# The last four blocks of a conditional-adapter kernel: b2 of block 126 by TensorE, block 125's last step by ScalarE and GpSimd, and two results stored in halves

## The chip, the cores and the metric

The kernel runs on one core of one Trainium2 chip. The metric is the time of one execution on the device in microseconds (us); lower is better. Three runs of the kernel before the change took 308.55, 308.73 and 308.92 us, so the median is 308.73 us. The core's engines are named as in the profile: PE is TensorE's matmuls and PEld its weight loads, DVE is VectorE, ACT is ScalarE, POOL is GpSimd, and SP is SyncE, which here only issues DMAs. "SPq" and "ACTq" stand for the instruction queues of SP and ACT when they issue a DMA.

## The reference

The input `x` holds 128 blocks of 128 rows by 512 columns in float32. Each block `b` has a language id from 0 to 9, and the id picks the block's own weights, biases, gamma and beta out of ten:

```
w1, w2 = W1[language_ids], W2[language_ids]
h = relu(einsum('bsh,bha->bsa', x, w1) + b1[language_ids][:, None, :])
adapted = einsum('bsa,bah->bsh', h, w2) + b2[language_ids][:, None, :]
y = x + adapted
mean = mean(y, axis=-1); var = mean(square(y - mean), axis=-1)
normed = (y - mean) * rsqrt(var + 1e-5)
out = x + normed * gamma[language_ids][:, None, :] + beta[language_ids][:, None, :]
```

H is 512, the inner width A is 128. All biases, gamma and beta are drawn, so none of them can be left out. One block's result is 128 x 512 float32, 256 KB, and the whole output is 33.55 MB.

## The kernel before, in words

The program is one loop over the 128 blocks, software-pipelined by hand: in iteration `i` TensorE transposes x of block `i`, multiplies block `i-1` with W1 ("down") and block `i-2` with W2 ("up"), and the other engines work on block `b = i-3` and its predecessors. Every instruction is put into its engine's queue by `keep`, which chains it behind the engine's last one, so the order within each engine is the order in which the program text is run. Between engines there are semaphore waits, which the framework adds from the tiles that each instruction reads and writes. Two engines that touch the same PSUM tile are ordered as well, also where both only read it.

The work on one block, with the lines that the profile names:

- TensorE: transposes (L235), `down` (L258), `up` (L275). For the blocks that `b2_by_matmul` names (5 and 127), a small bf16 matmul ahead of `up` puts b2 of the block into the PSUM tile first (L274).
- GpSimd: for the blocks that neither `b2_by_matmul` nor `b2_by_vector` names, `r = x + b2` (L245); for each block `o = x + beta` (L252), which starts the output tile.
- VectorE: `residual` (L292) adds `r`, or `x` itself where b2 is already in, to the PSUM tile and sums the rows; `scale` (L358) subtracts the mean and multiplies by gamma; `finish` (L367, and L424 in the tail) multiplies by the reciprocal deviation and adds the result to `o`.
- ScalarE: the square with its row sum (L315, in the tail L399), then an approximate reciprocal root (L325) that three small VectorE instructions refine (L329, L331, L334). ScalarE also copies xT and W1 and does the relu.

Row sums and means are kept for pairs of blocks: a [128, 2] tile `sums` for blocks 2g and 2g+1, and one small instruction, in the tail `negative_means` on VectorE (L299), for both means. It names the first block's PSUM tile as a second operand and does not use its values.

The last blocks are done by a tail of its own. `E` is 123. In the tail each block has its own deviation (`deviation_of`: square and root on ScalarE; `rstd_of(b, 1..3)`: the three steps on VectorE). Block 123 and 124 are finished by `by_pool`: ScalarE applies mean and deviation to the PSUM tile and writes `n` to SBUF (L413), GpSimd multiplies by gamma (L415) and adds `o` (L417). Block 125 is scaled on VectorE; its last step is shared: VectorE's `finish_cols` does columns 128 to 511 (L424), ScalarE and GpSimd columns 0 to 127 (L413, L417). Blocks 126 and 127 are finished by VectorE, 127 in two halves. Stores of single blocks (`store_last`, L420) are issued by SP, but those of 124 and 125 by ScalarE, behind its last computation. GpSimd's additions `x + beta` of blocks 124 to 127 stand behind `r` of block 126 in its queue, and the steps of `by_pool` behind them.

The part that the change touches is the call `tail(126)`, which runs after `up(127)` and lists the rest of the program in one order:

Of the kernel before, what the change touches and what calls it, by code (L numbers as in the profile page):

```python
# [12 lines left out]
ALU = mybir.AluOpType  # L13
# [13 lines left out]
def cond_resid_kernel(ctx: ExitStack, tc: tile.TileContext, x, itok, W1, b1, W2, b2, gamma, beta, out):  # L27
# [8 lines left out]
    nc = tc.nc  # L36
    B, S, H = x.shape
# [8 lines left out]
    def keep(ins):  # L46

        engine = ins.ins.engine
        if engine in last:
            tc.add_manual_dep(ins.ins, last[engine], behind, reason="kept order")  # L50
        last[engine] = ins.ins.name
        return ins
# [14 lines left out]
    E = B - 5  # L67
# [145 lines left out]
    xT, hT, rs, os, ys, ssqs, nmeans, rstds = {}, {}, {}, {}, {}, {}, {}, {}  # L213
# [1 line left out]


    def b2_by_matmul(b):
        return b in (5, B - 1)

    def b2_by_vector(b):  # L220
        return b < 4 or 8 <= b < B - 8 and (b % 4 == 1 if b < 24 else b % 16 in (1, 6, 11) or b % 32 == 30)
# [56 lines left out]
    def col(tiles, b):  # L278

        return tiles[b // 2][:, b % 2 : b % 2 + 1]  # L280
# [14 lines left out]
    def negative_means(g):  # L295

        nmeans[g] = st.tile([P, 2], FP, tag="nmean", name=f"nmean_{g}")
        keep(
            nc.vector.scalar_tensor_tensor(  # L299
                nmeans[g], sums[g], -1.0 / H, ys[2 * g][:, 0:2], ALU.mult, ALU.bypass  # L300
            )
        )
# [52 lines left out]
    def scale(b):  # L355
        v = lid(b, ET.DVE)
        keep(
            nc.vector.scalar_tensor_tensor(  # L358
                ys[b], ys[b], col(nmeans, b), gamma_b[:, bass.ds(v * H, H)], ALU.add, ALU.mult
            )  # L360
        )
# [15 lines left out]


    shifts = {}

    def of_one(b):
        if -b not in parts_of:
            pool, tag = {E + 3: (p_h, "h"), E + 4: (p_x, "xT")}.get(b, (p_s, "s"))
            parts_of[-b] = pool.tile([P, 1], FP, tag=tag, name=f"root_of_{b}"), st.tile([P, 1], FP, tag="part", name=f"part_of_{b}")
        return parts_of[-b]
# [10 lines left out]
    def deviation_of(b):  # L396
        ssqs[b] = st.tile([P, 1], FP, tag="ssq", name=f"ssq_{b}")
        sq = tp.tile([P, H], FP, tag="sq", name=f"sq_{b}")
        keep(nc.scalar.activation(sq, ys[b], AF.Square, bias=col(sums, b), scale=-float(H), accum_out=ssqs[b]))  # L399
        root(ssqs[b], of_one(b)[0])  # L400
# [8 lines left out]
    def by_pool(b, scaled, cols=slice(0, H)):  # L409

        n = rp.tile([P, H], FP, tag="r", name=f"n_{b}")[:, cols]
        bias = 0.0 if scaled else shifts[b]
        keep(nc.scalar.activation(n, ys[b][:, cols], AF.Identity, bias=bias, scale=rstd_col(b)))  # L413
        if not scaled:
            keep(nc.gpsimd.tensor_tensor(n, n, gamma_b[:, bass.ds(lid(b, ET.Pool) * H, H)], ALU.mult))  # L415
        o = os[b // 2][:, b % 2, cols]
        keep(nc.gpsimd.tensor_tensor(o, n, o, ALU.add))  # L417

    def store_last(b, engine=nc.sync, cols=slice(0, H)):
        keep(engine.dma_start(out=out[b][:, cols], in_=os[b // 2][:, b % 2, cols]))  # L420

    def finish_cols(b, cols=slice(0, H)):
        o = os[b // 2][:, b % 2, cols]
        keep(nc.vector.scalar_tensor_tensor(o, ys[b][:, cols], rstd_col(b), o, ALU.mult, ALU.add))  # L424

    def tail(b):
        p = E // 2
        residual(b)
        if b == E + 1:
            rstd(p, 1)  # L430
            scale(E - 1)
            rstd(p, 2)
            finish(E - 2)
            store(p - 1)
            rstd(p, 3)
            deviation_of(b)
            shift(E)
            by_pool(E, False)
        elif b == E + 2:
            rstd_of(b - 1, 1)  # L440
            negative_means(b // 2)
            rstd_of(b - 1, 2)
            finish_cols(E - 1)
            store_last(E - 1)
            rstd_of(b - 1, 3)
            store_last(E)
            deviation_of(b)
        elif b == E + 3:
            left, right = slice(0, H // 2), slice(H // 2, H)
            few, most = slice(0, H // 4), slice(H // 4, H)  # L450
            shift(b - 2)
            by_pool(b - 2, False)
            residual(b + 1)
            rstd_of(b - 1, 1)
            scale(b - 1)
            negative_means(b // 2)
            rstd_of(b - 1, 2)
            deviation_of(b)
            scale(b)
            rstd_of(b - 1, 3)  # L460
            rstd_of(b, 1)
            deviation_of(b + 1)
            rstd_of(b, 2)
            finish_cols(b - 1, most)
            by_pool(b - 1, True, few)
            store_last(b - 2, nc.scalar)
            store_last(b - 1, nc.scalar)
            rstd_of(b, 3)
            rstd_of(b + 1, 1)
            finish_cols(b)  # L470
            store_last(b)
            rstd_of(b + 1, 2)
            scale(b + 1)
            rstd_of(b + 1, 3)
            for cols in (left, right):
                finish_cols(b + 1, cols)
                store_last(b + 1, nc.sync, cols)
# [45 lines left out]
    for i in range(3, B + U):  # L523
        b = i - U - 1
# [111 lines left out]
```

## Time and profile before

| | us |
|---|---|
| median of three runs | 308.73 |
| lowest and highest run | 308.55 and 308.92 |
| span of the profiled execution, first to last instruction | 306.5 |
| PE busy | 294.6 |
| DVE busy | 295.9 |
| ACT busy | 282.3 |
| POOL busy | 283.9 |

The profile's page gives the profiled execution's span, 306.5 us, and no other time for it; the median of the runs is 2.23 us longer than that span. All four computing engines are busy for 92 to 97% of the span, on average over a long steady part and a short beginning and end. The change lies wholly in the end, the last 16 us. How to read the rows that follow: a row of the timeline has the start in us from the span's start, the length in us, the engine, the line, the operation, the tiles written and read, the shape, and in brackets the idle time of the engine before it and what ended that. A row of the chain of waits has start, length and what was being done or waited for. The numbers of blocks are not in the rows; they follow from the order. A row of DMA issues ends with the median time from issue to landing.

### The profile page before, as it was taken

How to read it: one execution, taken by the hardware profiler on the slowest of the kernel's cores; microseconds unless marked ns; L12 is line 12 of the kernel's file. 1: busy time of each engine (PE TensorE's matmuls, PEld its weight loads, DVE VectorE, ACT ScalarE, POOL GpSimd, SP SyncE). 2: the span in 40 equal slices, each digit the busy share in tenths (PEclk: the TensorE clock that was granted, in tenths of full speed). 3: DMA queues.
4: the chain of work that ended last, by engine and by line, in shares of the span. 5: the costliest groups of instructions: out<-in, count | busy, mean ns of one | idle time of the engine just before them, and what ended most of it. 6: DMA issues, size and time to landing. Idle time of an engine off the chain costs nothing. (4 is left out here: it accounts for less than half of the span.)

```text
span 306.5 us, 6981 instructions
## 1 busy us (share of the span) xinstructions
PE 294.6 (96%) x1835; PEld 220.0 (72%) x1835; DVE 295.9 (97%) x771; ACT 282.3 (92%) x777; POOL 283.9 (93%) x238
## 2 busy tenths in 40 slices
PE   8999999999999999999999999999999999999960
PEld 3748787777777777777777777777777777777730
DVE  6889999999999999999999999999999999999985
ACT  3858999999999999999999999999999999999981
POOL 1349899999999999999999999999999999999994
PEclk9999999999999999999999999999999999999995
DMA  6999999976678766766777666767776666773324
GB/s 231 379 390 388 373 371 354 387 231 240 221 255 276 250 202 241 226 257 219 259 276 243 213 209 238 265 224 260 275 238 206 226 231 242 246 266 137 135 109 171
DMA packets 43769, 77.85 MB, mean 254 GB/s; under 512 B 1961, under 2 KB 7348, under 8 KB 43730
## 3 DMA queue, kind: packets, MB, share of 16 engines
q1 hardware_dynamic: 43382, 76.84, 72.1%
q10 hardware_dynamic: 348, 0.57, 0.5%
q8 instruction: 15, 0.25, 0.3%
q14 instruction: 24, 0.20, 0.2%
HBM read 43.85 MB, written 33.55 MB: 253 GB/s over the span
## 5 line engine op out<-in xcount | busy, mean ns | idle before, releaser
L252 POOL TENSOR_TENSOR o<-x,beta_b 128x512 f32<-128x512 f32 x128 | 173.9, 1395 | 10.2 <-DVE beta_b L211 9.5
L245 POOL TENSOR_TENSOR r<-x,b_b 128x512 f32<-128x512 f32 x97 | 135.7, 1399 | 7.3 <-DVE b_b L211 6.2
L258 PE MATMUL ph<-xT,w1s 128*128 128x128 f32 x1024 | 135.4, 275 | 0.0
L275 PE MATMUL py<-w,hT 128*128 x256 | 131.2, 595 | 0.5 <-DVE b_b L211 0.5
L258 PEld LDWEIGHTS ph<-xT,w1s 128*128 128x128 f32 x1024 | 124.9, 192 | 1.0 <-ACT hT L266 0.5
L235 PEld LDWEIGHTS pxT<-ident,x 128*128 128x128 f32 x512 | 66.6, 151 | 65.3 <-issue 49.2
L358 DVE SCALAR_TENSOR_TENSOR py<-py,nmean,gamma_b 128x512 f32<-128x512 f32 x126 | 95.0, 754 | 0.9 <-ACT sq L399 0.8
L367 DVE SCALAR_TENSOR_TENSOR o<-py,rstd,o 128x512 f32<-128x512 f32 x122 | 91.2, 748 | 0.0
L315 ACT ACTIVATE sq<-py,sum 128x512 f32<-128x512 f32 x124 | 85.9, 693 | 2.8 <-DVE py L292 2.5
L235 PE MATMUL pxT<-ident,x 128*128 128x128 f32 x512 | 78.2, 276 | 0.0
L239 ACT COPY xT<-pxT 128x512 f32<-128x512 f32 x128 | 74.7, 584 | 3.5 <-PE pxT L235 3.5
L292 DVE SCALAR_TENSOR_TENSOR py<-py,r 128x512 f32<-128x512 f32 x97 | 67.0, 691 | 0.2
L226 ACT COPY w1s<-w 128x512 f32 x107 | 65.5, 612 | 0.0
L266 ACT ACTIVATE hT<-ph,b1T 128x128 f32<-128x128 f32 x128 | 46.9, 366 | 7.9 <-PE ph L258 2.6
L275 PEld LDWEIGHTS py<-w,hT 128*128 128x128 f32 x256 | 39.1, 192 | 2.9 <-issue 1.0
L315 ACT ACTIVATION_READ_ACCUMULATOR sq<-py,sum 128x1 f32 x124 | 25.0, 202 | 0.0
L292 DVE SCALAR_TENSOR_TENSOR py<-py,x 128x512 f32<-128x512 f32 x31 | 21.7, 699 | 0.4
L285 DVE TENSOR_TENSOR py<-py,b_b 128x512 f32<-128x512 f32 x29 | 20.2, 695 | 0.7 <-PE py L275 0.6
L325 ACT ACTIVATE root<-ssq,eps 128x2 f32<-128x2 f32 x62 | 16.4, 265 | 0.0
L292 DVE DVE_READ_ACCUMULATOR py<-py,r 128x1 f32 x97 | 13.7, 141 | 0.0
L306 ACT ACTIVATE nmean<-sum 128x2 f32<-128x2 f32 x62 | 12.3, 198 | 0.0
L329 DVE SCALAR_TENSOR_TENSOR part<-ssq,root 128x2 f32<-128x2 f32 x62 | 9.3, 151 | 0.2 <-ACT root L325 0.2
(55 smaller groups left out, 90.4 us busy)
## 6 DMA issues: line engine op xcount, KB each, us to landing
out_dram<-o SPq DMA_DIRECT2D x61, 512.0 KB, 3.4
x<-in_x_dram SPq DMA_DIRECT2D x29, 1024.0 KB, 6.2
x<-in_x_dram SPq DMA_DIRECT2D x6, 512.0 KB, 8.8
w1e<-in_L_cond_W_dram SPq DMA_DIRECT2D x2, 1280.0 KB, 12.3
w<-in_L_cond_W_dram SPq DMA_DIRECT2D x4, 640.0 KB, 8.1
w1s<-in_L_cond_W_dram SPq DMA_DIRECT2D x9, 256.0 KB, 8.4
w<-in_L_cond_W_dram SPq DMA_DIRECT2D x1, 1792.0 KB, 10.3
w<-in_L_cond_W_dram SPq DMA_DIRECT2D x1, 768.0 KB, 5.4
```

What stands on the lines that cost most here:

```text
L226: keep(nc.scalar.copy(w1s[b].rearrange("p k a -> p (k a)"), src))
L235: keep(nc.tensor.transpose(pxs[b][:, k, :], cols, ident))
L239: keep(nc.scalar.copy(xT[b], pxs.pop(b)))
L245: keep(nc.gpsimd.tensor_tensor(rs[b], xb(b), b2_b[:, bass.ds(v * H, H)], ALU.add))
L252: keep(nc.gpsimd.tensor_tensor(os[g][:, j, :], xb(b), beta_b[:, bass.ds(v * H, H)], ALU.add))
L258: nc.tensor.matmul(phs[b], lhsT=w1s[b][:, k, :], rhs=xT[b][:, k, :], start=(k == 0), stop=(k == KC - 1))
L266: keep(nc.scalar.activation(hT[b], phs.pop(b), AF.Relu, bias=b1T[:, bass.ds(lid(b, ET.Activation), 1)]))
L275: keep(nc.tensor.matmul(ys[b], lhsT=hT[b], rhs=w2[:, bass.ds(v * H, H)], start=not m, stop=True))
L292: nc.vector.scalar_tensor_tensor(ys[b], ys[b], 1.0, r, ALU.mult, ALU.add, accum_out=col(sums, b))
L315: nc.scalar.activation(sq, ys[b], AF.Square, bias=col(sums, b), scale=-float(H), accum_out=col(ssqs, b))
L358: nc.vector.scalar_tensor_tensor(ys[b], ys[b], col(nmeans, b), gamma_b[:, bass.ds(v * H, H)], ALU.add, ALU.mult)
L367: nc.vector.scalar_tensor_tensor(o, ys.pop(b), rstds[g][:, j : j + 1], o, ALU.mult, ALU.add)
```

## The change

There are four edits.

1. Block 126 joins 5 and 127 in `b2_by_matmul`. GpSimd no longer makes `r` for block 126, TensorE issues one more small matmul before `up(126)`, and VectorE's residual of block 126 reads `x`.
2. In `tail(126)`, `negative_means` of the pair 126 and 127 moves from ahead of `deviation_of(126)` (square and root of block 126) to behind it.
3. `finish_cols` of block 125 on VectorE goes away; `by_pool(125, True)` now does all 512 columns on ScalarE (one instruction instead of 128 columns) and GpSimd.
4. For blocks above 123, that is 124 and 125, `by_pool` makes GpSimd's last addition in two instructions of 256 columns each, and the stores of 124 and 125 on ScalarE's queue are issued in halves too: four stores of 128 KB instead of two of 256 KB.

```
     def b2_by_matmul(b):
-        return b in (5, B - 1)
+        return b in (5, B - 2, B - 1)
...
+    halves = slice(0, H // 2), slice(H // 2, H)
...
     def by_pool(b, scaled, cols=slice(0, H)):
...
-        o = os[b // 2][:, b % 2, cols]
-        keep(nc.gpsimd.tensor_tensor(o, n, o, ALU.add))
+        for part in halves if b > E else (cols,):
+            keep(nc.gpsimd.tensor_tensor(os[b // 2][:, b % 2, part], n[:, part], os[b // 2][:, b % 2, part], ALU.add))
...
             scale(b - 1)
-            negative_means(b // 2)
             rstd_of(b - 1, 2)
             deviation_of(b)
+            negative_means(b // 2)
             scale(b)
             rstd_of(b - 1, 3)
             rstd_of(b, 1)
             deviation_of(b + 1)
             rstd_of(b, 2)
-            finish_cols(b - 1, most)
-            by_pool(b - 1, True, few)
-            store_last(b - 2, nc.scalar)
-            store_last(b - 1, nc.scalar)
+            by_pool(b - 1, True)
+            for part in halves:
+                store_last(b - 2, nc.scalar, part)
+            for part in halves:
+                store_last(b - 1, nc.scalar, part)
             rstd_of(b, 3)
```

In this part of `tail`, `b` is 126. `few` and `most` (columns 0 to 127 and 128 to 511) are still defined, but no longer used.

## Prediction

> **What bounds the kernel now.** I read the page's head first, then the chain of waits from 299 us on, then the timeline of each engine over the last 16 us, and last the DMA views. All edits lie behind 290 us, and up to there the order on every engine is the same before and after, so only the end can change the time.
>
> ```profile
> span 306.5 us, 6981 instructions
> ```
>
> ```profile
> 301.69 0.42 POOLq L631
> ...
> 302.17 0.48 DVE o L424
> 302.65 0.39 DVEq L631
> ```
>
> The chain names GpSimd's end (302.11) as what released VectorE's last step, the two halves of block 127 at 302.17 and 302.57. I don't follow it there. The timeline of VectorE shows a nearer cause.
>
> ```profile
> 295.58 0.69 DVE L292 SCALAR_TENSOR_TENSOR py<-py,r 128x512 f32<-128x512 f32 x1
> ...
> 296.37 0.70 DVE L292 SCALAR_TENSOR_TENSOR py<-py,x 128x512 f32<-128x512 f32 x1
> ...
> 297.72 0.15 DVE L299 SCALAR_TENSOR_TENSOR nmean<-sum,py 128x2 f32<-128x2 f32 x1
> ...
> 298.73 0.76 DVE L358 SCALAR_TENSOR_TENSOR py<-py,nmean,gamma_b 128x512 f32<-128x512 f32 x1 [0.78 <-ACT sq L399]
> 299.39 0.15 DVE L334 SCALAR_TENSOR_TENSOR rstd<-part_of,root_of 128x1 f32<-128x1 f32 x1
> 299.46 0.15 DVE L329 SCALAR_TENSOR_TENSOR part_of<-ssq,root_of 128x1 f32<-128x1 f32 x1
> 299.64 0.16 DVE L331 SCALAR_TENSOR_TENSOR part_of<-part_of,root_of 128x1 f32<-128x1 f32 x1
> 299.73 0.62 DVE L424 SCALAR_TENSOR_TENSOR o<-py,rstd,o 128x384 f32<-128x384 f32 x1
> 300.26 0.15 DVE L334 SCALAR_TENSOR_TENSOR rstd<-part_of,root_of 128x1 f32<-128x1 f32 x1
> ...
> 300.51 0.75 DVE L424 SCALAR_TENSOR_TENSOR o<-py,rstd,o 128x512 f32<-128x512 f32 x1
> ...
> 301.90 0.15 DVE L334 SCALAR_TENSOR_TENSOR rstd<-part_of,root_of 128x1 f32<-128x1 f32 x1
> ```
>
> In order these are the residuals of 126 and 127, the means of their pair, the scaling of 126, the third step for 125, the first two for 126, the finish of 125 (columns 128 to 511), the third step for 126, the finish of 126, and the third step for 127. From 300.26 to the finish at 300.51 are 0.25 us, from 301.90 to 302.17 are 0.27: the last finish waits for VectorE's own step just as the one before it does, and GpSimd's end is a coincidence. So VectorE is busy without a gap from 298.73 to 303.04, and its start there hangs on ScalarE:
>
> ```profile
> 294.12 0.78 ACT L413 ACTIVATE n<-py,shift,rstd 128x512 f32<-128x512 f32 x1
> ...
> 296.50 0.78 ACT L413 ACTIVATE n<-py,shift,rstd 128x512 f32<-128x512 f32 x1 [0.38 <-DVE shift L407]
> 297.91 0.69 ACT L399 ACTIVATE sq<-py,sum 128x512 f32<-128x512 f32 x1 [0.64 <-DVE nmean L299]
> ...
> 299.72 0.27 ACT L325 ACTIVATE root_of<-ssq,eps 128x1 f32<-128x1 f32 x1
> 300.38 0.37 ACT L413 ACTIVATE n<-py,rstd 128x128 f32<-128x128 f32 x1 [0.40 <-DVE o L424]
> ```
>
> ScalarE makes n of 123 and 124, the square of 126 (idle 0.64 us for the means), the root of 127, and n of 125 (idle 0.40 for VectorE's finish of 125). The square doesn't use the means. It only reads the same PSUM tile as they do, and the same holds for n of 125 and the finish.
>
> Behind the last computation come the stores:
>
> ```profile
> 300.75:302.00 1.25, 0.50 0.00 0
> 302.00:305.00 3.00, 0.50 0.95 349
> ```
>
> ```profile
> 301.29 0.33 SPq L420 DMA_DIRECT2D out_dram<-o  x1
> ...
> 301.72 0.89 ACTq L420 DMA_DIRECT2D out_dram<-o  x2
> ...
> 303.10 0.59 SPq L420 DMA_DIRECT2D out_dram<-o  x1
> ```
>
> ```profile
> out_dram<-o SPq DMA_DIRECT2D x2, 256.0 KB, 2.0
> ...
> out_dram<-o SPq DMA_DIRECT2D x2, 128.0 KB, 2.3
> ```
>
> The columns of the first fence are window, length, TensorE's clock, DMA share and GB/s. No DMA runs from 300.75 to 302.00, then four blocks' results (1.05 MB: 126, 124, 125, and 127 in halves) leave at 349 GB/s until 305.0. The last store is issued at 303.10 and lands 2.3 us later, at 305.4, though it is only half as large as the stores that landed in 2.0. It stands in line behind the others. The span ends 1.1 us after that landing. So two things set the end: VectorE's last step, and 3 us of stores that all begin at 302.
>
> **The change, part by part.** *The square ahead of the means.* The square of 126 can start when n of 124 is done, 296.50 + 0.78 = 297.28, instead of 297.91. Scaling began 0.82 us after the start of the square (298.73 − 297.91) because it overwrites what the square reads. That would put it at 298.10. But in the new order the means wait for the square, and scaling needs the means. One small VectorE step behind another takes 0.18 us (299.46 to 299.64), so scaling starts at 298.28: 0.45 us earlier.
>
> The Trainium skill, page "PSUM — Partial Sum Buffer", section "PSUM bank collisions raise a hardware error", says that two engines must not touch one bank in the same partitions at the same time, two readers included, so that software has to order them. The trace agrees with its 0.64 us wait of a reader for a reader. By this rule the means wait and the sum below holds; without it they would stay at 297.72 and the end would come 0.18 us earlier still.
>
> *The finish of 125 leaves VectorE.* From the second step for 126 to its third are now 0.62 us (299.64 to 300.26), with the finish in between; without it they take 0.18. That is 0.44 earlier. The finish of 126 moves from 300.51 to 299.62, and what follows on VectorE is unchanged, so its end goes from 303.04 to 302.15: 0.89 us. ScalarE keeps up: root of 127 at 299.72 − 0.63 = 299.09, done at 299.36, and its first use was at 300.32 − 0.89 = 299.43 by the same shift.
>
> *n of 125 in one piece on ScalarE.* It needs the third step for 125, at 299.39 − 0.45 + 0.15 = 299.09, and ScalarE, free at 299.36. It takes 0.78 like the other n, until 300.14.
>
> *b2 of 126 by TensorE.* The nearest rows:
>
> ```profile
> 28.28 0.38 PE L274 MATMUL py<-parts,pick 96*128 96x512 bf16 x1
> 28.50 1.02 PE L275 MATMUL py<-w,hT 128*128 x2
> ```
>
> ```profile
> 293.96 1.02 PE L275 MATMUL py<-w,hT 128*128 x2
> 294.95 0.38 PE L274 MATMUL py<-parts,pick 96*128 96x512 bf16 x1
> 295.21 1.13 PE L275 MATMUL py<-w,hT 128*128 x2
> ```
>
> The small matmul costs 0.22 (block 5) to 0.26 us (block 127) between starts. Block 126's product, done at 294.98, moves to 295.20 or 295.24. VectorE takes it at 295.58, so 0.34 us of cover is left; if the cover were gone, all that follows would shift by the excess. Block 127's product is done at 296.34 and taken at 296.37, so there is no cover: its residual moves by 0 to 0.26 us. That is late for the means alone (297.72 to 297.98 at most), which now wait for the square until 298.10. I count nothing.
>
> *GpSimd.*
>
> ```profile
> 290.20 1.46 POOL L245 TENSOR_TENSOR r<-x,b_b 128x512 f32<-128x512 f32 x1
> 291.43 1.45 POOL L252 TENSOR_TENSOR o<-x,beta_b 128x512 f32<-128x512 f32 x1
> ...
> 296.34 1.45 POOL L415 TENSOR_TENSOR n<-n,gamma_b 128x512 f32<-128x512 f32 x1
> ...
> 299.08 1.26 POOL L415 TENSOR_TENSOR n<-n,gamma_b 128x512 f32<-128x512 f32 x1
> ...
> 300.43 1.27 POOL L417 TENSOR_TENSOR o<-n,o 128x512 f32<-128x512 f32 x1
> 301.65 0.46 POOL L417 TENSOR_TENSOR o<-n,o 128x128 f32<-128x128 f32 x1
> ```
>
> Without r of 126 all behind it moves up by 1.23 us (290.20 to 291.43). The multiplication for 123 moves to 295.11 (n is ready at 294.90), that for 124 to 297.85 (n ready at 297.28), the addition for 124 to 299.20. No row shows an addition of 256 columns. It lies between 0.46 and 1.27; in proportion to the columns between these two it is 0.73, which I take, as both ends are the same operation. The halves of 124 are then done at 299.93 and 300.66, those of 125 (n ready at 300.14) at 301.39 and 302.12. With 1.27 each the last would be at 304.3, with 0.46 GpSimd would wait for n and end at 301.1.
>
> *Stores.* ScalarE issues the halves of 124 at 300.14 (behind n of 125) and 300.66, those of 125 at 301.39 and 302.12; one issue takes 0.89 / 2 = 0.45, so they don't hold each other up. SP issues 126 at 301.29 − 0.89 = 300.40 and the last half of 127 at 303.10 − 0.89 = 302.21. Bytes flowed 0.71 us behind the first issue (301.29 to 302.00), so now from 300.85, and the same 1.05 MB at the same 349 GB/s take 3.0 us, to 303.85 if the line never runs empty. Landing comes 0.4 behind the bytes (305.0 to 305.4): 304.25. Another bound is the last issue: with the old delay of 2.3 it lands at 304.5, alone with half of a 256 KB store's 0.75 us saved from the 2.0 at 303.85. I take 304.3, 1.1 us earlier than now.
>
> **Sum.** 305.4 to 304.3 is −1.1 us; the span becomes 305.4. The profiled span is 2.23 us below the median of 308.73, and I leave that difference as it is: 307.6 us. The mechanism's own range is 307.2 (last store alone, 303.85) to 307.8 (old delay, 304.5).
>
> **Rivals.** *GpSimd's end decides*, as the chain reads it: VectorE's last finish waits for 302.12 instead of 302.11, and the time stays at 308.7. The 0.25 and 0.27 us above speak against it. *A wider GpSimd half*: at 1.27 each the last half store is issued at 304.3, and lands 1.7 us later at 306.0, 0.6 later than now: 309.3, slower. It needs more than 1.1 us per half to lose; the 128-column row at 0.46 speaks against it. *Partial loss*: a store line that starts early but runs empty, or TensorE's extra matmul with more than its 0.34 us of cover, would leave a gain of 0.3 to 0.6: 308.3.
>
> *Halved stores cost more than they bring.* If a half took as long on the DMA engines as a whole (0.75 us), the six halves and one whole would need 5.25 us from 300.85, land at 306.5 and give 309.8, slower. From 0.57 us per half on it is slower than now. The line of 302 to 305 with two halves in it still ran at 349 GB/s, which is 0.38 per half. The Trainium skill, page "DMA: Bandwidth & Descriptors", section "Rules for kernel authors", tells to coalesce small transfers into a large one, and so speaks for this rival. The 2.3 us of a 128 KB store beside 2.0 of a 256 KB one agree with it only on the face, since the later ones stood in line.
>
> **Chances.** The forecast 0.79; GpSimd's end 0.04; partial loss 0.09; a wide GpSimd half 0.03; dear halved stores 0.05. A measurement of this kernel can tell about 0.2%, 0.6 us, from no change. Faster is the forecast, 0.79; the same is GpSimd's end and the partial loss, 0.13; slower is the rest, 0.08. For 8 in 10 the range reaches from 307.2 into the partial loss, 308.4.
>
> **What would show it.** Right: the square of 126 follows n of 124 without idle time; the means follow the square and scaling starts near 298.3; VectorE ends near 302.1; the DMA share is high from about 300.9 to 303.9. Wrong: idle time of VectorE before the residual of 126, GpSimd halves over 0.9 us, a last store that lands over 2.5 us behind its issue, or a last finish that still starts just behind GpSimd's end.

## The result, and the profile after

The changed kernel takes 307.26 us (median of five runs, 306.69 to 307.67) where the kernel before takes 308.73 on the same chip (five runs, 308.48 to 308.97). The ratio is 0.9951, with a 95% interval of 0.9939 to 0.9963. The prediction was 307.6, faster. The profiled execution has a span 1.2 us shorter than that of before:

```profile
span 305.3 us, 6987 instructions
```

VectorE's timeline, from the residual of 126 on (the columns are those of the rows in the prediction):

```profile
295.61 0.69 DVE L292 SCALAR_TENSOR_TENSOR py<-py,x 128x512 f32<-128x512 f32 x1
...
296.39 0.70 DVE L292 SCALAR_TENSOR_TENSOR py<-py,x 128x512 f32<-128x512 f32 x1
...
297.74 0.15 DVE L331 SCALAR_TENSOR_TENSOR part_of<-part_of,root_of 128x1 f32<-128x1 f32 x1
298.00 0.16 DVE L299 SCALAR_TENSOR_TENSOR nmean<-sum,py 128x2 f32<-128x2 f32 x1
298.19 0.76 DVE L358 SCALAR_TENSOR_TENSOR py<-py,nmean,gamma_b 128x512 f32<-128x512 f32 x1
...
299.10 0.15 DVE L331 SCALAR_TENSOR_TENSOR part_of<-part_of,root_of 128x1 f32<-128x1 f32 x1
299.29 0.15 DVE L334 SCALAR_TENSOR_TENSOR rstd<-part_of,root_of 128x1 f32<-128x1 f32 x1
299.36 0.15 DVE L329 SCALAR_TENSOR_TENSOR part_of<-ssq,root_of 128x1 f32<-128x1 f32 x1
299.55 0.75 DVE L425 SCALAR_TENSOR_TENSOR o<-py,rstd,o 128x512 f32<-128x512 f32 x1
...
301.20 0.88 DVE L425 SCALAR_TENSOR_TENSOR o<-py,rstd,o 128x256 f32<-128x256 f32 x2
```

The two residuals are where they were, within 0.03 us (295.58 and 296.37 before). From there on VectorE gains twice: block 126 is scaled at 298.19 instead of 298.73, and its finish starts at 299.55 instead of 300.51, since the finish of 125 no longer stands between the second and third small step. VectorE ends at 302.08 instead of 303.04.

ScalarE and GpSimd:

```profile
296.52 0.78 ACT L414 ACTIVATE n<-py,shift,rstd 128x512 f32<-128x512 f32 x1 [0.38 <-DVE shift L408]
297.19 0.68 ACT L400 ACTIVATE sq<-py,sum 128x512 f32<-128x512 f32 x1
...
299.19 0.67 ACT L414 ACTIVATE n<-py,rstd 128x512 f32<-128x512 f32 x1
300.01 2.41 ACTq L421 DMA_DIRECT2D out_dram<-o  x4
```

```profile
289.12 6.26 POOL L252 TENSOR_TENSOR o<-x,beta_b 128x512 f32<-128x512 f32 x5
295.28 1.32 POOL L416 TENSOR_TENSOR n<-n,gamma_b 128x512 f32<-128x512 f32 x1
...
297.91 1.26 POOL L416 TENSOR_TENSOR n<-n,gamma_b 128x512 f32<-128x512 f32 x1
299.25 2.77 POOL L418 TENSOR_TENSOR o<-n,o 128x256 f32<-128x256 f32 x4
```

The square of 126 (297.19) has no idle time before it; before, it had 0.64. GpSimd makes the four halves from 299.25 to 302.02, and ScalarE issues their four stores from 300.01 on. Then the DMA side, first a table of windows (window, length, TensorE's clock, DMA share, GB/s), then the last half of 127 with its issue and the median time from issue to landing:

```profile
299.95:300.75 0.80, 0.55 0.00 0
300.75:304.00 3.25, 0.50 0.90 323
304.00:305.30 1.30, 0.50 0.00 0
```

```profile
302.14 0.39 SPq L421 DMA_DIRECT2D out_dram<-o  x1
```

```profile
out_dram<-o SPq DMA_DIRECT2D x1, 128.0 KB, 2.2
```

By these windows the stores start 1.25 us earlier than before (300.75 against 302.00) and the line is empty at 304.0 instead of 305.0. The last half is issued at 302.14 and lands 2.2 us later, at 304.4, where it landed at 305.4.

To compare executions below, one distance is used: from the start of VectorE's residual of block 127 (296.39 above) to the last landing. No edit moves that residual's place in the order, and an execution that starts a little earlier or later as a whole does not change the distance. It was 9.06 us in the profile of before and is 7.99 in this one (the landings are taken from the trace's completion records to two digits): a gain of 1.07.

### The profile page after: what moved, and what is told of

The parts are those of the page before. It is cut to its first block, busy times and chain, and to the rows that moved or that the text cites. A ratio compares the mean times of both kernels' runs of the same rounds, so it can differ in the third digit from the quotient of the medians.

```text
span 305.3 us, 6987 instructions
## 1 busy us (share of the span) xinstructions
PE 294.6 (97%) x1836; PEld 220.2 (72%) x1836; DVE 295.5 (97%) x770; ACT 282.1 (92%) x777; POOL 283.7 (93%) x239
## 4 chain that ended last, share of the span: by engine, by line
PE 92%; DVE 5%; issue 1%; ACT 1%; DVEq 0%; POOL 0%; ACTq 0%; POOLq 0%
PE ph L258 36%; PE py L275 34%; PE pxT L235 18%; PE row L206 2%; DVE py L358 2%; PE idle L486 1%; DVE py L292 1%; DVE o L367 1%; DVE b_b L211 0%; ACT n L414 0%; ACT sq L315 0%; ACT sq L400 0%; DVE o L425 0%; ACT w1s L226 0%; DVE rstd L334 0%
## 5 line engine op out<-in xcount | busy, mean ns | idle before, releaser
L252 POOL TENSOR_TENSOR o<-x,beta_b 128x512 f32<-128x512 f32 x128 | 163.7, 1294 | 10.5 <-DVE beta_b L211 9.5
L245 POOL TENSOR_TENSOR r<-x,b_b 128x512 f32<-128x512 f32 x96 | 124.3, 1295 | 7.1 <-DVE b_b L211 6.2
L292 DVE SCALAR_TENSOR_TENSOR py<-py,x 128x512 f32<-128x512 f32 x32 | 22.4, 699 | 0.4
```

What stands on the lines that cost most here:

```text
L245: keep(nc.gpsimd.tensor_tensor(rs[b], xb(b), b2_b[:, bass.ds(v * H, H)], ALU.add))
L252: keep(nc.gpsimd.tensor_tensor(os[g][:, j, :], xb(b), beta_b[:, bass.ds(v * H, H)], ALU.add))
L292: nc.vector.scalar_tensor_tensor(ys[b], ys[b], 1.0, r, ALU.mult, ALU.add, accum_out=col(sums, b))
```

## The experiments

All medians in one place. "Ratio" is against the kernel before, run on the same chip beside it, with its 95% interval; "distance" is the one just defined; "GpSimd" is where GpSimd's first instruction behind `x + beta` (n of 123 times gamma) starts, counted from the same residual. Span, distance and GpSimd are those of one profiled execution of each kernel; that of the changed kernel took 307.08 us, 0.18 below its median. The four undone kernels have runs of the kernel before of their own beside them (308.68, against 308.73 beside the changed kernel), so a difference of two medians below compares two groups of runs.

| kernel | median (range), us | ratio | span | distance | GpSimd |
|---|---|---|---|---|---|
| before, profile of the start | 308.73 | 1 | 306.5 | 9.06 | -0.04 |
| before_again (one run) | 308.47 | | 306.7 | 9.06 | 0.15 |
| after | 307.26 (306.69 to 307.67) | 0.9951 (0.9939 to 0.9963) | 305.3 | 7.99 | -1.11 |
| u_means: without edit 2 | 307.70 (307.20 to 307.80) | 0.9965 (0.9953 to 0.9978) | 305.9 | 8.64 | -0.41 |
| u_b2: without edit 1 | 308.46 (307.65 to 308.63) | 0.999 (0.998 to 0.9999) | 306.7 | 9.20 | 0.58 |
| u_finish: without edit 3 | 307.41 (307.02 to 307.72) | 0.996 (0.9947 to 0.9973) | 305.4 | 8.41 | -0.67 |
| u_halves: without edit 4 | 307.72 (307.61 to 307.85) | 0.997 (0.9959 to 0.9981) | 305.9 | 8.44 | -0.38 |
| only_b2: before with edit 1 alone | 307.89 (307.78 to 308.21) | 0.9981 (0.9972 to 0.999) | 306.1 | 9.07 | -0.45 |
| no_stores: after, four stores left out | 306.46 (one run) | | 304.7 | 7.54 | -0.43 |
| inter | 307.62 (306.88 to 307.67) | 0.9962 (0.995 to 0.9974) | 305.9 | 8.65 | -0.46 |
| six_o | 306.69 (306.29 to 307.14) | 0.9938 (0.9924 to 0.9951) | 305.3 | 7.88 | -1.40 |
| six_o_inter | 307.39 (306.87 to 307.77) | 0.9963 (0.9951 to 0.9976) | 305.1 | 8.12 | -1.38 |
| six_o_before | 307.94 (307.59 to 308.34) | 0.998 (0.9971 to 0.9989) | 306.1 | 9.06 | -0.31 |
| late_pool | 308.92 (308.66 to 309.28) | 1.001 (1.0 to 1.0019) | 307.3 | 9.92 | 1.92 |

**u_means: the means back ahead of the square (edit 2 undone).**

```
             scale(b - 1)
+            negative_means(b // 2)
             rstd_of(b - 1, 2)
             deviation_of(b)
-            negative_means(b // 2)
             scale(b)
```

> The changed kernel with edit 2 alone undone: the means of the pair 126/127 stand ahead of block 126's square again. My theory: ScalarE idles some 0.6 us for the means again, VectorE scales block 126 near 298.7 instead of 298.19 and ends near 302.6 instead of 302.08; ScalarE's first half store comes behind n of 125, near 300.7 instead of 300.01. The last landing goes from 304.38 to about 304.9, the span from 305.3 to about 305.8, the time 0.5 us above the changed kernel's. Rival, that the line of stores alone sets the end and VectorE's last step doesn't: the start of the line moves too, by 0.5 to 0.7 us, so this run can't tell the two apart, but with no loss of time both would be wrong.

The timeline of VectorE in that kernel, then that of ScalarE:

```profile
298.70 0.76 DVE L358 SCALAR_TENSOR_TENSOR py<-py,nmean,gamma_b 128x512 f32<-128x512 f32 x1 [0.78 <-ACT sq L400]
...
301.77 0.88 DVE L425 SCALAR_TENSOR_TENSOR o<-py,rstd,o 128x256 f32<-128x256 f32 x2
```

```profile
297.89 0.69 ACT L400 ACTIVATE sq<-py,sum 128x512 f32<-128x512 f32 x1 [0.63 <-DVE nmean L299]
```

The waits of before are back, 0.63 on ScalarE and 0.78 on VectorE. The scaling starts at 298.70 instead of 298.19 and VectorE's last finish at 301.77 instead of 301.20, 0.57 later. So the order of two readers of one PSUM tile, of which neither uses what the other computes, is worth about half a microsecond at VectorE's end. The median rises by 0.44 us (the intervals of the ratios overlap) and the distance by 0.65, but how much of either is the edit's is not shown: GpSimd, on which the edit changes nothing, stood 0.70 later beside VectorE in this execution (-0.41 against -1.11), and `inter` below, with GpSimd in the same place and VectorE's end 0.96 earlier than here, has the same distance.

**u_b2: r of 126 by GpSimd again (edit 1 undone).**

```
     def b2_by_matmul(b):
-        return b in (5, B - 2, B - 1)
+        return b in (5, B - 1)
```

> The changed kernel with edit 1 alone undone: GpSimd makes r of block 126 again, TensorE has one small matmul fewer. My theory: everything on GpSimd behind r moves back by 1.2 us, its end from 302.02 to about 303.25, ScalarE's last half store is issued near 303.3 and lands near 305.1, so that the span is about 306.0 and the time 0.7 us above the changed kernel's; VectorE's last finish stays at 301.2. Rival, that GpSimd's end releases VectorE's last finish, as the chain of waits of the kernel before has it: VectorE's last finish moves to 303.3, the last landing to about 306.4, the time 2 us above the changed kernel's.

VectorE's last row of that kernel, and the kernel's chain of waits in order of time:

```profile
301.24 0.88 DVE L425 SCALAR_TENSOR_TENSOR o<-py,rstd,o 128x256 f32<-128x256 f32 x2
```

```profile
...
299.83 1.22 POOL n L416
301.05 0.05 issue
301.10 0.76 POOLq L633
301.85 2.04 POOL o L418 x3
303.92 0.34 ACTq L421 DMA_DIRECT2D out_dram<-o  x1
```

VectorE's last finish stays at 301.24 although GpSimd now works until 303.90. So the finish does not wait for GpSimd, which settles the prediction's first rival. But the time is nearly that of before (308.46, ratio 0.999; 1.20 above the changed kernel where I expected 0.7): the last store is now ScalarE's, issued at 303.92, 1.9 us behind the 302.05 of the changed kernel. Not all of GpSimd's delay is the edit's: its work stands 1.69 later beside VectorE, and r of 126 costs 1.23. Undoing edit 1 alone can take nearly the whole gain away, but not in each execution: three of the twelve runs took 307.65 to 307.71.

**u_finish: VectorE does columns 128 to 511 of block 125 again (edit 3 undone).**

```
-            by_pool(b - 1, True)
+            finish_cols(b - 1, most)
+            by_pool(b - 1, True, few)
...
-            for part in halves:
-                store_last(b - 1, nc.scalar, part)
+            store_last(b - 1, nc.scalar)
```

(with it, GpSimd's addition of block 125 is one instruction of 128 columns again, so that block 125 is no longer in halves)

> The changed kernel with edit 3 alone undone: VectorE finishes columns 128 to 511 of block 125 again, ScalarE and GpSimd the first 128; block 125 is stored whole, block 124 in halves. My theory: VectorE's end moves by 0.44 us, from 302.08 to 302.5, GpSimd ends near 301.1. The last store is issued near 302.6 and lands near 304.7 in a line that started near 301.0: span 305.6, time 0.2 to 0.4 us above the changed kernel's. Rival, that GpSimd's and ScalarE's part is what counts (GpSimd has 1 us less here): the time is the changed kernel's or up to 0.3 us below it.

VectorE's residual of 127 and its last finish in that kernel:

```profile
296.03 0.70 DVE L292 SCALAR_TENSOR_TENSOR py<-py,x 128x512 f32<-128x512 f32 x1
...
301.27 0.88 DVE L426 SCALAR_TENSOR_TENSOR o<-py,rstd,o 128x256 f32<-128x256 f32 x2
```

The whole execution was 0.36 us early (its residual of 127 starts at 296.03). Beside that residual VectorE's last finish starts 5.24 us later (301.27 - 296.03) against 4.81 (301.20 - 296.39) in the changed kernel: 0.43, where the prediction's term is 0.44. The distance rises by 0.42: the last half of 127 is issued 6.18 behind the residual (302.21 - 296.03) instead of 5.75 (302.14 - 296.39) and lands 2.23 later, as in the changed kernel; GpSimd had ended 1.0 us before that issue. The median rises by 0.15 alone, with intervals that overlap widely (0.996 against 0.9951). So the trace shows the term at its predicted size and the times can't tell whether all of it arrives.

**u_halves: GpSimd's last two results and their stores in whole blocks (edit 4 undone).**

```
-            for part in halves:
-                store_last(b - 2, nc.scalar, part)
-            for part in halves:
-                store_last(b - 1, nc.scalar, part)
+            store_last(b - 2, nc.scalar)
+            store_last(b - 1, nc.scalar)
```

(and the additions on GpSimd in one instruction of 512 columns each)

> The changed kernel with edit 4 alone undone: GpSimd adds blocks 124 and 125 in one instruction each, and ScalarE stores each whole. My theory: GpSimd ends near 301.7 instead of 302.02 (two additions of 1.26 us instead of four of 0.72), the line of stores starts near 301.05 with block 126 instead of 300.8, and runs full until about 304.1: last landing 304.4 to 304.6, span 305.3 to 305.5, the time within 0.2 us of the changed kernel's. Rival, that halved stores cost more on the DMA engines than whole ones: the line is shorter by more than 0.25 us and the time 0.3 us or more below the changed kernel's. Other rival, that the early start of the line was worth its whole 0.3 to 0.5 us: time that much above it.

The table of windows for that kernel:

```profile
300.75:301.25 0.50, 0.50 0.39 152
301.25:301.75 0.50, 0.50 0.94 365
301.75:302.00 0.25, 0.50 0.06 17
302.00:302.50 0.50, 0.50 0.89 340
...
304.00:304.50 0.50, 0.50 0.43 160
```

I expected hardly any effect, and the median rises by 0.46 us, the distance by 0.45. The rows show where the time of this execution went: block 126 fills the line from about 301.0 to 301.75, then it is nearly empty until 302.00, because ScalarE can't store block 124 before GpSimd has made all of it and issues that store at 301.17 instead of 300.01. From 302.00 on the line is full again, to about 304.3, and the last store is ScalarE's whole block 125, issued at 302.39. But GpSimd stood 0.73 later beside VectorE in this execution (-0.38 against -1.11), and without that, by an estimate from these rows, both of ScalarE's stores would have been issued 0.73 earlier and there would have been no gap. So the 0.45 can't be put down to the halves. All seven runs, 307.61 to 307.85, lie above the changed kernel's median, but the intervals of the two ratios still touch (0.9959 to 0.9981 and 0.9939 to 0.9963). What the halves bring remains open; that they cost time no run shows.

**no_stores: what the line itself costs.** The stores of blocks 124 and 125 are left out.

```
-            for part in halves:
-                store_last(b - 2, nc.scalar, part)
-            for part in halves:
-                store_last(b - 1, nc.scalar, part)
```

> The changed kernel without the four half stores of blocks 124 and 125; those two blocks are computed but not written out. It prices the line of stores: my theory says that the last half of 127, issued near 302.14, lands 2.24 us later because it stands behind 124 and 125, and alone it lands after 1.7 to 1.8 us, near 303.9: span about 304.8 instead of 305.3. Rival, that the last issue alone decides: landing near 304.3 and a span of 305.2 to 305.3.

The issue of the last half of 127 in that kernel:

```profile
301.71 0.38 SPq L421 DMA_DIRECT2D out_dram<-o  x1
```

It lands at 303.50 by the completion records, 1.79 us behind its issue, where the same store in the changed kernel takes 2.24. So 0.45 us of the changed kernel's end is still a store that stands behind others, and the distance falls by as much (7.99 to 7.54).

**only_b2: edit 1 alone.**

```
-        return b in (5, B - 1)
+        return b in (5, B - 2, B - 1)
```

> The kernel before with edit 1 alone: b2 of block 126 by TensorE. Undoing edit 1 cost most of the gain (308.46 against 308.68 before), so the question is whether it brings the gain by itself. My theory, that GpSimd's end and VectorE's end have to move together: GpSimd ends 1.2 us earlier, near 301 to 301.4, block 124 is stored near 300.8, but VectorE still ends near 303.0 and issues its last store near 303.1, which lands 1.8 to 2.0 us later, near 305.0: time 0.4 to 0.7 us below the kernel before, near 308.1. Rival, that edit 1 is the change: about 307.3, and edits 2 to 4 bring nothing.

In its profile the distance is that of before, 9.07: GpSimd is earlier, VectorE's end and the stores behind it are not. The landing comes near 305.0, as I expected, but only because the whole execution was early. Its median is nevertheless 0.76 below that of before on the same chip (308.65, 22 runs). Between the two profiled executions the whole difference lies ahead of the tail: the residual of 127 starts 0.4 earlier (295.99 against 296.37, see the last section). The rest of the 0.76 is what late_pool looks into.

**late_pool: GpSimd delayed, in the kernel before.** The left half of r of 126 is added twice.

```
             add_b2(b + 3)
+            half_r = slice(0, H // 2)
+            b2_row = b2_b[:, bass.ds(lid(b + 3, ET.Pool) * H, H)]
+            keep(nc.gpsimd.tensor_tensor(rs[b + 3][:, half_r], xb(b + 3)[:, half_r], b2_row[:, half_r], ALU.add))
             add_beta(b + 1)
```

> The kernel before with one more GpSimd instruction: the left half (256 columns) of r of block 126 is added twice with the same result, so that all of GpSimd's work behind it comes 0.73 us later (the 256-column addition took 0.72 us). Nothing else is changed. My theory: in most executions of the kernel before GpSimd already stands later than in its two profiles, and both the first store of ScalarE and the last one then count for the end, so that not only VectorE's last finish sets it. Then the delay shows in the time: median 309.1 to 309.4 us (+0.4 to +0.7), and in the profile the last landing comes 9.3 to 9.8 us behind VectorE's residual of block 127 (9.06 in the kernel before), with VectorE's own steps unmoved, the two last finishes 6.6 us behind that residual or nearly so. Rival: VectorE's end alone sets the time of the kernel before, with up to a microsecond to spare on GpSimd. Then the median stays at 308.6 within 0.2, and the landing at 9.06.

VectorE's last row in that kernel, and the kernel's chain of waits:

```profile
301.98 0.88 DVE L424 SCALAR_TENSOR_TENSOR o<-py,rstd,o 128x256 f32<-128x256 f32 x2
```

```profile
...
300.72 1.22 POOL n L415
...
301.99 1.30 POOLq L634
303.29 0.41 POOL o L417
```

VectorE's last finish starts 5.79 us behind the residual of 127 (301.98 - 296.19), as before (302.17 - 296.37 = 5.80). GpSimd stands 1.96 later than in the profile of before, 0.73 of it by the added instruction and the rest by longer waits early on (last section). The chain runs through GpSimd alone, which ends at 303.71, and the distance is 9.92. So a late GpSimd does set the end through ScalarE's stores while VectorE is unmoved: the rival is refuted as to the mechanism. The size is not what I expected: 308.92 against 308.69 on the same chip is 0.23, at the edge of the interval, and not 0.4 to 0.7. In this profile the last landing comes 2.40 us behind GpSimd's end (306.11 - 303.71). A distance of 9.06 is therefore reached when GpSimd ends 6.66 behind the residual; in the profile of before it ended 5.74 behind (302.11 - 296.37), with 0.9 to spare. Either the median executions of before have some of that to spare, too, or they start later than this one, whose residual of 127 stands 0.18 and 0.40 earlier than in the two profiles of before (296.19 against 296.37 and 296.59); otherwise 0.73 more would have cost 0.73. What makes only_b2 0.76 faster in the median while its distance stays at 9.07 remains open: no execution of before as slow as its median was profiled.

**inter: VectorE's end earlier still.** In the changed kernel, the scaling of 127 moves ahead of the finish of 126, so that the small steps of both blocks lie between large ones.

```
             deviation_of(b + 1)
+            scale(b + 1)
             rstd_of(b, 2)
+            rstd_of(b + 1, 1)
             by_pool(b - 1, True)
...
             rstd_of(b, 3)
-            rstd_of(b + 1, 1)
-            finish_cols(b)
-            store_last(b)
             rstd_of(b + 1, 2)
-            scale(b + 1)
             rstd_of(b + 1, 3)
+            finish_cols(b)
+            store_last(b)
```

> The changed kernel with VectorE's last steps in another order: block 127 is scaled right behind the first small step of block 126, so that the small steps of 126 and 127 no longer wait for one another in a row. The same instructions, no work left out. My theory, that VectorE's last step and the line of stores set the end together: VectorE's end moves from 302.08 to about 301.65, block 126 is stored later, near 300.9, the last landing goes from 304.38 to about 304.0, where ScalarE's last half store, issued at 302.05, takes over; time 0.2 to 0.4 us below the changed kernel's. Rival, that the line alone sets the end: the same bytes start no earlier, and the time stays within 0.1 us or rises, because block 126 comes later.

VectorE's last three steps, the finish of 126 and the two of 127, run in one piece:

```profile
299.96 1.53 DVE L425 SCALAR_TENSOR_TENSOR o<-py,rstd,o 128x512 f32<-128x512 f32 x3
```

VectorE ends at 301.49, 5.33 behind its residual of 127 (296.16) where the changed kernel has 5.69, a gain of 0.36. None of it arrives: 307.62. The store of 126 starts later, GpSimd is still at work until 302.44, and the last store is ScalarE's, issued at 302.47. That is not yet the rival's case: GpSimd stood 0.65 later in this execution than in the changed kernel's (-0.46 against -1.11), and it set the last store. six_o_inter below parts the two.

**six_o and its two companions: GpSimd's early wait taken away.** Near 52 us GpSimd waits for the landing of an output store, since there are five output tiles. A sixth is given, paid for with one tile each of two other pools.

```
-    op = ctx.enter_context(tc.tile_pool(name="op", bufs=5))
+    op = ctx.enter_context(tc.tile_pool(name="op", bufs=6))
...
-        hT[b] = tp.tile([P, P], FP, tag="hT", name=f"hT_{b}", bufs=6)
+        hT[b] = tp.tile([P, P], FP, tag="hT", name=f"hT_{b}", bufs=5)
...
-        sq = tp.tile([P, H], FP, tag="sq", name=f"sq_{b}")
+        sq = tp.tile([P, H], FP, tag="sq", name=f"sq_{b}", bufs=1)
```

> The changed kernel with six output tiles instead of five; to make room, one square tile instead of two and five hT tiles instead of six. In the profiles so far GpSimd waits once, near 52 us, for the landing of an output store, for 0.5 to 1.0 us, and from there on it runs without a wait to the end, so that its distance from VectorE at the end is what that one wait left. My theory, that this one wait is why GpSimd's end and so the time differ from one execution to the next: the wait goes, GpSimd's additions for blocks 124 to 127 begin 0.5 to 1.0 us earlier beside VectorE's steps, GpSimd ends at 301.7 or earlier instead of 302.02, the runs spread less, and the median falls by 0.2 to 0.4 us below the changed kernel's 307.26. Rival, that the spread comes from elsewhere: median and spread stay.

GpSimd's waits from 28 to 290 us (what waited, for what, total, times, longest), of the changed kernel and then of six_o:

```profile
POOL r L245 <- DMA x<-in_x_dram: 0.9, 1, 0.9
POOL o L252 <- DMA out_dram<-o: 0.8, 1, 0.8
```

```profile
POOL r L245 <- DMA x<-in_x_dram: 1.0, 1, 1.0
POOL r L245 <- DVE py L292: 0.2, 1, 0.2
```

The wait for the output store is gone. At the end GpSimd now waits for ScalarE instead:

```profile
295.09 1.27 POOL L416 TENSOR_TENSOR n<-n,gamma_b 128x512 f32<-128x512 f32 x1 [0.29 <-ACT n L414]
```

The median is 306.69, the lowest of all kernels here that write every result, 0.57 below the changed kernel. The two ratios (0.9938 and 0.9951) come from two groups of runs and their intervals overlap, so this is likely but not certain. Its distance is 0.11 shorter, in the slowest of its runs (307.14), which is the one profiled. The spread of its runs (0.85 us) is hardly below the changed kernel's (0.98).

The same sixth tile on the kernel before:

> The kernel before with six output tiles (and the same smaller tiles as in the run of the changed kernel with six). It asks how much of that run's 0.6 us comes from GpSimd's wait near 52 us, independent of the change. My theory, that the end of the kernel before is a line of stores which GpSimd's end and VectorE's end feed together: GpSimd ends 0.5 to 1 us earlier, VectorE's last step stays; time 0.2 to 0.5 us below the kernel before. Rival, that GpSimd's lead is worth its whole length in both kernels: 0.6 to 1.0 us below. Other rival, that the gain came from something else than GpSimd: no difference.

307.94, 0.71 below the before on the same chip, where I expected 0.2 to 0.5, and again with an unchanged distance (9.06) in its profile; the same open point as in only_b2.

And with the order of inter on top of six_o:

> The changed kernel with both: six output tiles, and VectorE's last steps interleaved. In the interleaved run VectorE ended 0.4 us earlier beside its own steps, but GpSimd's end (302.44) and ScalarE's last half store (302.47) took over. My theory: with GpSimd 0.5 to 1 us earlier too, the last issue is near 301.8 and the last landing near 304.0; time 306.3 to 306.6, below the 306.69 of six output tiles alone. Rival, that the line of 1.05 MB from 300.8 on, at 340 GB/s, ends at 303.9 whatever the engines do: no more than 0.1 us below 306.69.

307.39, where I expected 306.3 to 306.6; it is above six_o alone, though on another chip and with intervals that meet at 0.9951. The profiles make a clean pair: GpSimd stands in the same place (-1.38 and -1.40), VectorE ends 0.36 earlier beside its residual, and the distance is 0.24 longer (8.12 against 7.88). The line of stores in it:

```profile
300.75:301.25 0.50, 0.50 0.72 254
301.25:301.75 0.50, 0.50 0.70 266
```

Block 126 is finished and stored later in this order, so the line, which began early, is not full here. The last half of 127 is issued at 301.47 and lands 2.65 us later by the completion records, against 2.24 in the changed kernel: it only stands in line longer. With both engines early, the stores set the end, as the rival of `inter` had it.

The kernel before, profiled once more:

> The kernel before, profiled once more. Its first profile had a span of 306.5, 2.23 us below the median of its runs, while the changed kernel's five runs all lie 1.76 to 1.80 us above their spans. My theory: the first profile caught an execution with GpSimd early (additions of blocks 124 to 127 from 290.20 + 1.23). A typical one has a span near 306.9, its multiplication for block 123 starts 0.3 to 0.7 us later than 296.34 beside VectorE's same steps, and GpSimd waits longer near 52 us. Rival: the profile is again like the first one, and the difference between runs lies outside the span.

Its distance is 9.06 again, and its run took 308.47 us with a span of 306.7, so 1.77 above the span: the 2.23 of the first profile was no gap outside the span. GpSimd stands 0.19 later than in the first profile, less than the 0.3 to 0.7 expected, and the 0.2 us that the span is longer are there before the tail: the residual of 127 starts at 296.59 instead of 296.37 (last section).

## Why the prediction was right

**The square ahead of the means.** The prediction put the square at 297.28, the means behind it, and the scaling at 298.28; the trace has 297.19, 298.00 and 298.19. The means, which could have followed the small step at 297.74, started 0.26 us later than that, at 298.00, when the square and the reading of its row sum (to 297.96) were over. The trace agrees with the rule of the Trainium skill, page "PSUM — Partial Sum Buffer", section "PSUM bank collisions raise a hardware error", that two readers of one bank have to be kept apart by software: the means waited for the square although neither writes the tile. What would happen without the wait no run here shows.

**The finish of 125.** The finish of 126 was to start at 299.62 and VectorE to end at 302.15; they are 299.55 and 302.08. The total of 0.89 came as 0.96. Undone one at a time, the two parts gave 0.57 and 0.43.

**n of 125.** Predicted at 299.36 for 0.78 us. It started at 299.19 and took 0.67: the rows of 123 and 124, from which the 0.78 was taken, read a third tile (shift), and this one doesn't.

**TensorE's extra matmul.** Counted at nothing, and the two residuals indeed start within 0.03 us of their old places: the matmul took 0.22 us (293.98 to 294.20) of the 0.34 to spare.

```profile
293.98 0.38 PE L274 MATMUL py<-parts,pick 96*128 96x512 bf16 x1
294.20 1.02 PE L275 MATMUL py<-w,hT 128*128 x2
```

**GpSimd.** The interpolated 0.73 for a half was 0.69 between starts (2.77 for four). The multiplication for 123 started 0.17 late (295.28 for 295.11), without waiting for ScalarE: GpSimd as a whole was that late, its first `x + beta` in the rows above starting at 289.12 where before has 288.96. The shorter halves made up for it. The end of 302.12 was 302.02. That it came so close is partly luck: in the six other kernels with five output tiles and the same work on GpSimd up to there (u_means, u_finish, u_halves, only_b2, no_stores, inter) it stood 0.44 to 0.73 later beside VectorE, and the prediction had no term for that.

**Stores.** ScalarE's four issues were put at 300.14 to 302.12 and stand at 300.01 to 302.05, SP's last at 302.21 and stands at 302.14. The line ended near 304.0, 0.15 later than the 303.85 predicted; it did not run empty in between. (The 323 GB/s instead of 349 are the mean of a window whose first quarter of a microsecond is only 0.28 busy; from 301.00 to 304.00 the share is 0.80 to 1.06.) The landing at 304.38 lies inside the bounds of 303.85 to 304.5, beside the 304.3 taken. The lower bound was too low: without the stores of 124 and 125 the last half still takes 1.79 us (no_stores), which from 302.21 is 304.0.

**The sum.** 305.4 was predicted for the span, 305.3 came; the landing came 1.0 earlier than before (1.07 beside the residual) where 1.1 was predicted.

**The term that was mis-sized: the 2.23 us between span and median**, which was left as it was. In every later profile the time of the profiled execution itself is known, and it lies 1.73 to 1.84 us above its span (307.08 and 305.3 for the changed kernel, 308.47 and 306.7 for before_again). The first profile of before had no such time beside it. With 1.77 it took about 308.27, so it was an execution 0.46 quicker than the median. Counted with 1.77 the prediction would have read 307.2 for an execution like the profiled one, and 307.08 came. The term made the forecast 0.46 too high for such an execution, and the 307.6 lies 0.34 above the median. Against the median of before the kernel gained 1.47, against its profile in distance 1.07; the 0.4 between them were in no term, and may belong to what only_b2 leaves open. The range of 307.2 to 308.4 held the median, 0.06 above its lower end.

**The rivals.** *GpSimd's end decides*: u_b2 refutes it as put, since VectorE's last finish stood still with GpSimd 1.88 us later. But the step behind it, that GpSimd's end at 302.11 was a coincidence without weight, is only right while GpSimd has time to spare: by its stores GpSimd did set the end in u_b2, inter and late_pool. *A wider GpSimd half*: refuted, 0.69. *Partial loss*: the line did not run empty and TensorE's cover held; standing in line still costs the last store 0.45 (no_stores). *Halved stores cost more than they bring*: the six halves and one whole were through 3.25 us after 300.75, not 5.25, and u_halves, with whole stores, was not faster. The Trainium skill, page "DMA: Bandwidth & Descriptors", section "Rules for kernel authors", tells to coalesce small transfers, and the figure in that row is 64 KB, below which a transfer is mostly overhead; these pieces are 128 KB. No run here shows a loss by cutting the 256 KB stores, whose line still moved 323 GB/s. That the halves themselves bring time is not shown either (u_halves).

## What to carry to other kernels

At a kernel's end several chains finish together, here VectorE's steps, GpSimd's steps and the line of stores; shortening one gains only down to the next (only_b2 moved GpSimd alone, six_o_inter beside six_o VectorE alone, and the distance didn't shrink), and undoing one can take nearly the whole gain away (u_b2). When two engines read one PSUM tile, put the reader that the path needs first, and look in the trace for idle time whose releaser computes nothing that the waiter uses. Before a difference of some tenths of a microsecond is forecast against a median, find out where the profiled execution itself stands among the runs.

## What the runs showed that I had not expected

**GpSimd carries delays from 32 and 52 us to the end.** The waits of GpSimd between 28 and 290 us in late_pool:

```profile
POOL r L245 <- DMA x<-in_x_dram: 1.9, 1, 1.9
POOL o L252 <- DMA out_dram<-o: 1.1, 1, 1.1
```

It waits twice, for a load of x near 32 us and for an output store near 52 us, and then never again until the tail. What it loses there, 1.7 us in the changed kernel (0.9 + 0.8) and 3.0 here, it doesn't make up in 240 us. Its place in the tail follows these waits: with 1.7 us of them it is -1.11 (the changed kernel), with 2.3 to 2.8 it is -0.67 to -0.38 (the six others with the same work: u_means, u_finish, u_halves, only_b2, no_stores, inter). Between executions its place in the tail beside VectorE differed by up to 0.7 us among kernels with the same work on it (-1.11 in the changed kernel, -0.41 and -0.46 in u_means and inter). That is as much as one edit is worth, so the order of kernels whose medians differ by 0.2 us, such as after and u_finish, is not settled here.

**The start differs, and most of the difference reaches the end.** ScalarE's first copy of xT, in the changed kernel and in only_b2:

```profile
6.53 0.58 ACT L239 COPY xT<-pxT 128x512 f32<-128x512 f32 x1 [2.94 <-PE pxT L235]
```

```profile
6.12 0.59 ACT L239 COPY xT<-pxT 128x512 f32<-128x512 f32 x1 [2.54 <-PE pxT L235]
```

No edit touches that part. VectorE's residual of 127 starts at 296.39 in the one and at 295.99 in the other, so the 0.41 is still 0.40 there; six_o_before and six_o_inter have the same two times as only_b2. In eleven of the fourteen profiles the residual comes 289.83 to 289.91 us behind the first copy; in late_pool, no_stores and six_o it comes up to 0.3 later (no_stores: copy at 5.84, residual at 295.97). The program need not differ for that: the kernel before itself has the copy at 6.52 in its first profile and at 6.69 in before_again, and the residual at 296.37 and 296.59. Whether it belongs to an execution or to a kernel as it was loaded can't be told from these profiles; if it belongs to the kernel as loaded, it is a part of what only_b2 and six_o_before gained.
